# A recommender kernel with 16384 lookups a position: which tiles of rows are gathered whole, and which row by row

## The chip, the core and the metric

The kernel runs on one core of a Trainium2 chip. The metric is the device time of one execution in microseconds. The program is one launch: 200 history positions, then two small dense layers, all in float32.

## The reference

`B = 16384` samples, `L = 200` history positions, embeddings of `D = 64` floats (256 bytes a row). Cut to what is computed:

```python
it, c, u = i_emb[item], c_emb[cate], u_emb[user]        # each (B, 64)
h = i_emb[hist]                                         # (200, B, 64)
feat = concat([h, it, h - it, h * it])                  # (200, B, 256)
a = dice(feat @ au_W1 + au_b1, au_alpha, axis=1)        # 36 units; moments over the batch, for each l
w = a @ au_W2 + au_b2                                   # (200, B, 1)
cur = sum(w * h, axis=0)                                # (B, 64)
z = concat([u, it, c, cur])                             # (B, 256)
z = dice(z @ W1 + b1, alpha1, axis=0)                   # 80 units
z = dice(z @ W2 + b2, alpha2, axis=0)                   # 40 units
out = z @ W3 + b3                                       # (B, 2)
# dice(x) = x * (p + alpha * (1 - p)),  p = sigmoid((x - mean) / sqrt(var + eps))
```

The item, category and user tables are read by random index: 16384 rows for each of 200 positions, which is 3.3 million rows of 256 bytes.

## The kernel before

**Tiles and steps.** A tile is 128 samples (one row of the table for each partition). The batch is 128 tiles, cut in `ND = 8` groups of `TD = 16` tiles. A step `k = 8 l + c` handles group `c` of history position `l`: 16 tiles of rows are brought into `rows[k % 5]` (five buffers, L105), DVE turns them into `hT` by 32x32 blocks (L153, four instructions a step), PE multiplies, ACT evacuates `xs` (`hidden`, L372) and computes the sigmoid (`gate`, L361), DVE multiplies and adds to `curT` (L364, L368, L369). `gate`, `weights` and `weigh` of a step come `LAG = 9` steps late, when the moments of their position are known (`moments`, L403).

**Two ways of fetching rows.** A whole tile comes by one indirect DMA, which POOL issues from a column of 128 indices in SBUF (`gather`, L124; here "a gather"). For the groups in `SIDES = (1, 3, 4, 5, 6, 7)` the sixteenth tile can come by address instead: SP and ACT load 128 row addresses into registers, up to 24 at a time (L315), and each issues half of them as a DMA of 256 bytes (L323; here "a row DMA"), into one of three `side` buffers. DVE waits until all 128 have landed (`await_rows`, L342) and copies the tile into `rows` (`place_tile`, L385). `shares` (L293) spreads the row DMAs of a position evenly over its 8 steps: with 5 tiles by address each queue issues 40 a step, with 6 tiles 48. On ACT they stand between `hidden` and `gate` and behind `gate` (`step`, L423).

**How many tiles by address.** Five groups always have one; group 5 (`SOMETIMES`) has one where `l % EACH < MOST` (`has_side`, L348). With `EACH = 3` that is every third position. A position with 6 such tiles costs POOL 122 gathers, here "a six"; one with 5 costs 123 gathers, "a five". Before, the order is six, five, five.

**Stages.** (1) The start: the item rows are gathered, group by group, into `rows[c % 5]` and turned into `itT` (L538 to L554); with `ask_all` six tiles come by address, with 432 row DMAs on SP and 336 on ACT. Beside that the categories are looked up by matrix products: DVE compares (`pick_categories`, L498: 8 comparisons for each of 16 half groups), PE multiplies, ACT copies each half out of PSUM (L509), and ACT's queue loads and stores (`spread_categories`, `store_categories`). History step `k` fills `rows[k % 5]`, so step 0 needs the item group 5 turned, step 1 group 6. Memsets and copies end the stage (L556 to L566); `head_weights` (L246, 57 small DMAs on SP, then DVE operations that wait for them) is called last, and most of it is placed behind the loop. (2) The loop: 2 passes of `LPB = 90` positions (L570), with a barrier of all engines between passes and behind the last. (3) 20 positions more. (4) The users (L645 to L675): 8 groups, 122 + 1 gathers and 5 tiles by address, and the first dense layer for each group: `head_layer` multiplies category, item and `curT` (into `px`, 128 rows, and `ph`, 32 rows), then the user rows come in, and ACT evacuates (`head_units`). The last attention steps (`gate`, `weights`, `weigh`) run in between. (5) Two dense layers with moments over the whole batch (L677 to L750).

**Order.** `manual_schedule` keeps the order of the program on each engine within a region; the engines meet through semaphores alone.

Of the kernel before, what the change touches and what calls it, by code (L numbers as in the profile page):

```python
# [14 lines left out]
P = 128  # L15
# [12 lines left out]
EACH = 3  # L28
# [8 lines left out]
def din_kernel(  # L37
# [76 lines left out]
    ids = [make(f"ids{i}", P, NC, dt=I32) for i in range(2)]  # L114
    side = [make(f"side{i}", P, D) for i in range(3)]
# [117 lines left out]
    w2b = make("w2b", P, P)  # L233
    w3 = make("w3", P, 4, P)
    b1a = make("b1a", P, 1)
    b1b = make("b1b", S, 1)
# [9 lines left out]
    def head_weights():  # L246
# [9 lines left out]
        for g in range(2):  # L256

            nc.sync.dma_start(w1a[ts(g, D), 2, ts(g, ZA)], w1[:, 2, :ZA])
            nc.sync.dma_start(w1b[ts(g, D), 2, ts(g, ZB)], w1[:, 2, ZA:])
            nc.sync.dma_start(w2a[ts(g, ZA), g * ZA : g * ZA + Z2], W2[:ZA])  # L260
            nc.sync.dma_start(b1a[ts(g, ZA)], col(b1)[:ZA])
            nc.sync.dma_start(ala[ts(g, ZA)], col(alpha1)[:ZA])
            nc.sync.dma_start(b1b[ts(g, ZB)], col(b1)[ZA:])
            nc.sync.dma_start(bias2[g * ZA : g * ZA + Z2], col(b2))
            nc.sync.dma_start(al2[g * ZA : g * ZA + Z2], col(alpha2))
            for j in range(4):
                r = slice(j * S + g * ZB, j * S + (g + 1) * ZB)
                nc.sync.dma_start(w2b[r, g * ZA : g * ZA + Z2], W2[ZA:])
                w = j * S + g * ZO
                nc.sync.dma_start(w3[g * ZA : g * ZA + Z2, j, w : w + ZO], W3)  # L270
                nc.sync.dma_start(alb[r], col(alpha1)[ZA:])
        nc.sync.dma_start(bias3, b3.partition_broadcast(P))
# [64 lines left out]
    def ask_all(s, split, first, n, at, table):  # L337
        for queue, runs in enumerate(shares(NS * P // ND, s, split)):
            runs = [(r0, min(end, n * P)) for r0, end in runs if r0 < n * P]
            ask(queue, runs, first, range(n), at, table)  # L340

# [47 lines left out]
    def fetch_all(k, c, ids, table):  # L389
        for n in range(TD - (c in SIDES)):  # L390
            j = column(c, n)
            gather(rows[k % ROWS], ids[:, j : j + 1], n, table)
# [91 lines left out]
    def order_categories():  # L484
        for c in range(ND):
            n, j = TD - (c in SIDES), column(c, 0)
            nc.scalar.dma_start(cs[c][:, :n], columns(r_cate)[:, j : j + n])
            if c in SIDES:
                j = column(c, TD - 1)
                nc.scalar.dma_start(cs[c][:, n:], col(r_cate[j * P : (j + 1) * P]))  # L490
        nc.scalar.dma_start(table, c_emb.rearrange("(b p) d -> p b d", p=PB))
# [26 lines left out]
    with tc.manual_schedule():  # L518
        nc.sync.dma_start(ids[0], columns(r_item))
        load_addresses(2, r_item.rearrange("(o b) -> o b", o=1))  # L520
        nc.vector.memset(hm, 0.0)
        nc.scalar.copy(hT[SPREAD], hm)
        order_categories()
        load_hist_ids(0, 0)
        load_addresses(0, r_hist[0:1])
        nc.sync.dma_start(ids[1], columns(r_user))
        nc.gpsimd.iota(lanes, pattern=[[1, P]], base=P, channel_multiplier=-1)
        for q in range(SPREAD - 1):
            spread_categories(q)
# [4 lines left out]
        scale_addresses(2)  # L534
# [3 lines left out]
        for c in range(ND + 1):  # L538
            if c < ND:
                fetch_all(c, c, ids[0], i_emb)  # L540
                ask_all(c, 0.56, -NS, NS, addr[2], i_emb)
                for q in (2 * c, 2 * c + 1):
                    pick_categories(q)
                    if q + SPREAD - 1 < HALVES:
                        spread_categories(q + SPREAD - 1)
                    if q:
                        store_categories(q - 1)
            if c == 0:
                attention_weights()
                scale_addresses(0)  # L550
            if c:
                if c - 1 in SIDES:
                    place_tile(c - 1, SIDES.index(c - 1) - NS)
                transpose(itT[c - 1], rows[(c - 1) % ROWS])  # L554
# [12 lines left out]
        head_weights()  # L567
# [10 lines left out]
    zst = [make(f"zst{i}", P, n, STATS) for i, n in enumerate((2 * ND, 4, 2 * ND))]  # L578

    def measure_head(i, j, t, h):  # L580
        nc.vector.bn_stats(zst[i][:, 2 * j + h, :], t[:, ts(h, CH)])

# [34 lines left out]
    def head_layer(pairs):  # L617
        layer(px, [(w1a[:, f], t) for f, t in pairs], last=False)
        layer(ph[:S], [(w1b[:, f], t) for f, t in pairs], last=False)
# [6 lines left out]
    def head_units(c):  # L626
        evacuate(za[c], px, b1a, 0, c)
        if c == ND - 1:
            start_moments("z", 0, 2, 0, same_a)
        for h in range(2):  # L630
            nc.scalar.activation(
                zb[c // 4][ts(c % 4, S), ts(h, CH)], ph[:S, ts(h, CH)], AF.Identity, bias=b1b
            )
            if c % 4 == 3:
                measure_head(1, c // 4, zb[c // 4], h)

    with tc.manual_schedule():
        steps(BODY, L - BODY, L - BODY, r_user.rearrange("(o b) -> o b", o=1))
        U = addr[(L - BODY) % 3]
        j = column(SIDES[-1], TD - 1)  # L640
        nc.sync.dma_start(sidx[0], col(r_user[j * P : (j + 1) * P]))
        first = -(-tiles_by_address(L - BODY)[0] // 3) * 3

        weighed = {*range(-LAG, K - LAG), K, K + 1}
        for j in range(ND + 2):  # L645
            if j < ND:
                fetch_all(K + j, j, ids[1], u_emb)
                if j == SIDES[-1]:
                    gather(rows[(K + j) % ROWS], sidx[0], TD - 1, u_emb)
                nc.sync.dma_start(category[j % 2], catT[j])  # L650
            step(K + j, K - 1, weighed)
            weighed.add(K + j - LAG)
            left = [k for k in range(K) if k not in weighed]
# [5 lines left out]
            if j < ND:  # L659
                ask_all(j, SPLIT, first, NS - 1, U, u_emb)  # L660
            if 1 <= j <= ND:
                c = j - 1
                head_layer(((2, category[c % 2]), (1, itT[c]), (3, curT[c])))
                if c in SIDES[:-1]:
                    place_tile(K + c, first + SIDES.index(c))
                parts = (0, TD) if c < ND - 1 else (0, TD - 4, TD)
                for n in map(slice, parts, parts[1:]):
                    transpose(user[c % 2], rows[(K + c) % ROWS], n)
                    for dst, w in ((px, w1a[:, 0]), (ph[:S], w1b[:, 0])):
                        for i in range(2):  # L670
                            nc.tensor.matmul(
                                by_tile(dst, i)[:, n], w, by_tile(user[c % 2], i)[:, n],
                                start=False, stop=n.stop == TD, skip_group_check=True,
                            )
# [21 lines left out]

        beside = {0: range(4), 4: range(4, 6), 6: range(6, 8)}
        for c in range(ND + 2):
            if c < ND:
                if c % 4 == 0:  # L700
                    dice(ab[c // 4], zb[c // 4], nb, al1b, alb, 2 if c == 0 else 1, c > 0)
                for i in range(2):
                    for k in beside.get(c, ()):
                        r = ts(k % 4, S)
                        nc.tensor.matmul(
                            pz[k % 4][:, ts(i, CH)], w2b[r], ab[k // 4][r, ts(i, CH)],
                            start=True, stop=False, skip_group_check=True,
                        )
                dice(curT[c], za[c], na, al1a, ala, 2 if c == 0 else 1, c % 2 == 1)
                layer(pz[c % 4], [(w2a, curT[c])], first=False)  # L710
# [70 lines left out]
```

## Time and profile before

| what | before |
|---|---|
| median of 3 runs | 31195.79 us (31191.82 to 31199.41) |
| the profiled execution | 31199.79 us |
| its span, first to last instruction | 31198.0 us |
| POOL: busy, instructions | 23418.8 us (75%), 24783 |
| gathers: item, history, user | 122, 24533, 123 |
| PE, DVE, ACT busy | 67%, 50%, 12% |
| row DMAs on SP and on ACT | 69056 and 68928 |
| granted TensorE clock, mean | 0.809 |

The profiled execution lies 4.0 us above the median. The page counts only the execution of instructions as busy: the issuing of a DMA by SP or ACT, and POOL's time between two gathers, stand as idle. So POOL's 75% and ACT's 12% aren't the load of these engines. In the lists, "start us, us" are the start and length of a group of instructions, and the bracket holds the idle time before it and what ended it; "ACTq" and "SPq" are the queues' own instructions. A name stands without its buffer number.

### The profile page before, as it was taken

Reading aid. Unit: us, or ns where it says so; the run is one execution under the profiler, and the core shown is the slowest. Engines: PE = TensorE matmul, PEld = TensorE weight load, DVE = VectorE, ACT = ScalarE, POOL = GpSimd, SP = SyncE. Lnnn points to the kernel's source line nnn. Section 1 sums busy time; section 2 is a strip of 40 time slices with the busy share of each in tenths; the row PEclk is TensorE's granted clock in tenths of the full one; section 3 lists DMA queues with packets and bytes.
Section 4 is the critical chain, followed back from the end, with each engine's and each line's share of the span. In section 5 each row is a group of like instructions: output and inputs, shape, how many; then the busy total and the mean of one; then the engine's idle time right before and its main releaser. Section 6 shows DMA issues by size and latency. Waiting matters only on the chain.

```text
span 31198.0 us, 427397 instructions
## 1 busy us (share of the span) xinstructions
PE 20922.2 (67%) x39376; PEld 8551.5 (27%) x39376; DVE 15705.3 (50%) x21745; ACT 3823.8 (12%) x3330; POOL 23418.8 (75%) x24783
## 2 busy tenths in 40 slices
PE   5666666666666666666666666666666666666667
PEld 2222222222222222222222222222222222222222
DVE  4555554554555555555455455555555555545554
ACT  1111111111111111111111111111111111111111
POOL 6777777777777777777777777777777777777776
PEclk7888888888888888888888888887888888888888
DMA  2111111111111111111111111111111111111111
GB/s 41 29 29 29 29 29 29 29 29 29 29 29 29 29 29 29 29 29 29 29 29 29 29 29 29 29 29 29 29 29 29 29 29 29 29 29 29 29 29 30
DMA packets 1135469, 907.51 MB, mean 29 GB/s; under 512 B 730704, under 2 KB 730704, under 8 KB 1132426
## 3 DMA queue, kind: packets, MB, share of 16 engines
q0 software_dynamic: 792896, 813.51, 13.9%
q1 hardware_dynamic: 193404, 35.89, 0.8%
q10 hardware_dynamic: 146125, 30.64, 0.7%
q14 instruction: 2734, 22.39, 0.2%
q8 instruction: 310, 5.08, 0.1%
HBM read 873.55 MB, written 4.39 MB: 28 GB/s over the span
## 4 chain that ended last, share of the span: by engine, by line
POOL 32%; issue 12%; PE 5%; DMA 4%; DVE 2%; ACTq 1%; ACT 0%; DVEq 0%; POOLq 0%
POOL rows L125 32%; DMA rows<-in_L_rec_i_emb,idx 4%; PE px L158 2%; PE ph L158 1%; PE wb L158 1%; ACTq L323 1%; DVE hT L153 1%; DVE wb L368 0%; DVE curT L369 0%; ACT pg L361 0%; DVE st L377 0%; ACTq L315 0%; ACT xs L372 0%; DVE y L364 0%; DVE hm L400 0%
## 5 line engine op out<-in xcount | busy, mean ns | idle before, releaser
L125 POOL DMA_INDIRECT rows<-in_L_rec_i_emb,idx x24400 | 23038.6, 944 | 7542.4 <-issue 7198.7
L158 PE MATMUL ph<-hT,unit 128*128 128x512 f32 x6404 | 5928.7, 1077 | 9820.7 <-DVE hT L153 9820.2
L368 DVE SCALAR_TENSOR_TENSOR wb<-wb,au_bias,hT 128x1024 f32<-128x1024 f32 x1609 | 2080.3, 1293 | 9802.6 <-PE wb L158 9802.6
L158 PEld LDWEIGHTS ph<-hT,unit 128*128 128x128 f32 x6404 | 1747.3, 305 | 12865.9 <-DVE hT L153 12687.8
L153 DVE STREAM_TRANSPOSE hT<-rows 64x512 f32<-64x512 f32 x6404 | 4517.0, 705 | 1483.9 <-DMA rows<-in_L_rec_i_emb,idx 894.5
L158 PE MATMUL px<-hT,blk_h 128*128 128x512 f32 x6404 | 4125.0, 733 | 0.0
L372 ACT ACTIVATE xs<-px,au_bias 128x1024 f32<-128x1024 f32 x1602 | 1783.6, 1113 | 14375.2 <-PE wb L158 10720.9
L158 PE MATMUL wb<-y,blk_p 128*128 128x512 f32 x6436 | 3318.4, 597 | 246.6 <-DVE y L364 246.1
L361 ACT ACTIVATE pg<-xs,sh,rs 128x1024 f32<-128x1024 f32 x1609 | 1943.0, 1208 | 12481.6 <-issue 9985.6
L158 PE MATMUL px<-itT,blk_i 128*128 128x512 f32 x6404 | 3355.8, 606 | 0.0
L158 PE MATMUL wb<-xs,blk_x 128*128 128x512 f32 x6436 | 3300.5, 594 | 5.3 <-DVE curT L369 5.3
L158 PE MATMUL px<-hm,blk_m 128*128 128x512 f32 x6408 | 3011.2, 592 | 0.0
L400 DVE TENSOR_TENSOR hm<-ph,itT 128x1024 f32<-128x1024 f32 x1601 | 1960.6, 1225 | 1920.1 <-PE ph L158 1920.0
L364 DVE TENSOR_TENSOR y<-pg,xs 128x1024 f32<-128x1024 f32 x1609 | 1959.4, 1218 | 1293.7 <-ACT pg L361 1291.5
L158 PEld LDWEIGHTS px<-hT,blk_h 128*128 128x128 f32 x6404 | 1649.9, 258 | 2417.9 <-issue 2363.7
L377 DVE BATCH_NORM_STATS2 st<-xs 128x6 f32<-128x512 f32 x3204 | 2058.9, 685 | 60.8 <-ACT xs L372 17.1
L369 DVE TENSOR_TENSOR curT<-wb,curT 128x1024 f32<-128x1024 f32 x1609 | 1970.4, 1225 | 54.8
L158 PEld LDWEIGHTS px<-itT,blk_i 128*128 128x128 f32 x6404 | 1402.0, 219 | 2031.2 <-issue 2031.2
L158 PEld LDWEIGHTS wb<-y,blk_p 128*128 128x128 f32 x6436 | 1215.2, 191 | 1847.9 <-issue 1460.7
L158 PEld LDWEIGHTS wb<-xs,blk_x 128*128 128x128 f32 x6436 | 1224.6, 190 | 1551.9 <-issue 1544.4
L158 PEld LDWEIGHTS px<-hm,blk_m 128*128 128x128 f32 x6408 | 1217.4, 190 | 1532.9 <-issue 1520.3
L387 DVE COPY rows<-side 128x64 f32<-128x64 f32 x1079 | 235.7, 218 | 485.0 <-DMA side<-in_L_rec_i_emb 472.9
(184 smaller groups left out, 2044.3 us busy)
## 6 DMA issues: line engine op xcount, KB each, us to landing
side<-in_L_rec_i_emb SPq DMA_DIRECT2D x68720, 0.2 KB
side<-in_L_rec_i_emb ACTq DMA_DIRECT2D x68624, 0.2 KB
rows<-in_L_rec_i_emb,idx POOLq DMA_INDIRECT x24400
idx<-in_r_hist SPq DMA_DIRECT2D x200, 61.0 KB
hT<-cs ACTq DMA_DIRECT2D x16, 500.0 KB
side<-in_L_rec_u_emb SPq DMA_DIRECT2D x336, 0.2 KB
side<-in_L_rec_u_emb ACTq DMA_DIRECT2D x304, 0.2 KB
ucT<-catT SPq DMA_DIRECT2D x8, 512.0 KB
```

Source lines behind the costliest of these rows:

```text
L125: nc.gpsimd.indirect_dma_start(out=dst[:, n, :], out_offset=None, in_=table, in_offset=bass.IndirectOffsetOnAxis(ap=ids, axis=0),)
L153: nc.vector.transpose(by_tile(dst[ts(e, D)], i)[:, n], of[ts(i, D), n, ts(e, S)])
L158: nc.tensor.matmul(dst[:, ts(i, CH)], lhsT, rhs[:, ts(i, CH)], start=(first and j == 0), stop=(last and j == len(pairs) - 1), skip_group_c ...
L323: dma = issue.dma_start(side[m % 3].bitcast(U8)[p : p + 1], flat[ds(a, ROW)].rearrange("(o d) -> o d", o=1),).then_inc(landed[m % 3], 16)
L361: nc.scalar.activation(pg, xs[k % XR], AF.Sigmoid, bias=shifts[i], scale=rstds[i])
L364: nc.vector.tensor_mul(y, pg, xs[k % XR])
L368: nc.vector.scalar_tensor_tensor(wb, wb, au_bias2, hT[k % LAG], ALU.add, ALU.mult)
L369: nc.vector.tensor_add(curT[k % ND], wb, curT[k % ND])
L372: nc.scalar.activation(xs[k % XR], px, AF.Identity, bias=au_bias)
L377: nc.vector.bn_stats(stats[l % 3][:, 2 * c + i, :], xs[k % XR][:, ts(i, CH)])
L387: nc.vector.tensor_copy(rows[k % ROWS][:, TD - 1], side[m % 3])
L400: nc.vector.tensor_mul(hm, ph, itT[k % ND])
```

## The change

1. **Items whole.** All 128 item tiles are gathered by POOL; `ask_all` and the row DMAs of the items go. Column indices of the six tiles come by `load_all_ids`, six small DMAs on SP.
2. **The order of the start.** The loads of the category indices are interleaved with the first `spread_categories`; the loads of history position 0 move behind the attention weights; the user indices and `head_weights` move into the item loop, at group 2.
3. **Users.** 126 gathers and only two tiles by address (groups 3 and 5), all on SP. The loop has one round less. `head_layer` is split: category and item come before `gate`/`weights`/`weigh`, `curT` and user behind. Its 32-row part (`ph`) is packed: four products of 256 columns side by side in the four quarters of the partitions in place of two of 512 in one quarter, so that one ACT instruction of 128x256 evacuates it.
4. **The second layer** takes the packed part 256 columns at a time, each group for itself, behind the main product.
5. **`EACH = 2`**: the sixth tile comes by address in every second position. The order is six, five, six, five.

```diff
-EACH = 3
+EACH = 2
...
+    side_ids = [make(f"side_ids{i}", P, NS, dt=I32) for i in range(2)]
...
-    w2b = make("w2b", P, P)
+    w2b = make("w2b", P, 2, P)
...
-    b1b = make("b1b", S, 1)
+    b1b = make("b1b", P, 1)
...
-    def fetch_all(k, c, ids, table):
-        for n in range(TD - (c in SIDES)):
+    def load_all_ids(i, v):
+        for s in range(NS):
+            j = NC + s
+            nc.sync.dma_start(side_ids[i][:, s : s + 1], col(v[j * P : (j + 1) * P]))
+
+    def fetch_all(k, c, i, table, by_address=()):
+        for n in range(TD):
             j = column(c, n)
-            gather(rows[k % ROWS], ids[:, j : j + 1], n, table)
+            at = ids[i][:, j : j + 1] if j < NC else side_ids[i][:, j - NC : j - NC + 1]
+            if j - NC not in by_address:
+                gather(rows[k % ROWS], at, n, table)
...
-        load_addresses(2, r_item.rearrange("(o b) -> o b", o=1))
+        load_all_ids(0, r_item)
...
-        order_categories()
-        load_hist_ids(0, 0)
-        load_addresses(0, r_hist[0:1])
-        nc.sync.dma_start(ids[1], columns(r_user))
         nc.gpsimd.iota(lanes, pattern=[[1, P]], base=P, channel_multiplier=-1)
-        for q in range(SPREAD - 1):
-            spread_categories(q)
+        for c in range(3):
+            order_categories(c)
+        nc.scalar.dma_start(table, c_emb.rearrange("(b p) d -> p b d", p=PB))
+        for c in range(3, ND):
+            if c - 3 < SPREAD - 1:
+                spread_categories(c - 3)
+            order_categories(c)
...
             if c < ND:
-                fetch_all(c, c, ids[0], i_emb)
-                ask_all(c, 0.56, -NS, NS, addr[2], i_emb)
+                fetch_all(c, c, 0, i_emb)
...
             if c == 0:
                 attention_weights()
+                load_hist_ids(0, 0)
+                load_addresses(0, r_hist[0:1])
                 scale_addresses(0)
+            if c == 2:
+                nc.sync.dma_start(ids[1], columns(r_user))
+                load_all_ids(1, r_user)
+                head_weights()
             if c:
-                if c - 1 in SIDES:
-                    place_tile(c - 1, SIDES.index(c - 1) - NS)
                 transpose(itT[c - 1], rows[(c - 1) % ROWS])
...
-        head_weights()
...
-    def head_layer(pairs):
-        layer(px, [(w1a[:, f], t) for f, t in pairs], last=False)
-        layer(ph[:S], [(w1b[:, f], t) for f, t in pairs], last=False)
+    def head_layer(pairs, first=False, last=False, n=(0, TD)):
+
+        for i in range(2):
+            for j, (f, t) in enumerate(pairs):
+                nc.tensor.matmul(
+                    by_tile(px, i)[:, slice(*n)], w1a[:, f], by_tile(t, i)[:, slice(*n)],
+                    start=first and j == 0, stop=last, skip_group_check=True,
+                )
+        for j, (f, t) in enumerate(pairs):
+            for r in range(4):
+                n0 = r % 2 * TD // 2
+                of = slice(max(n[0], n0), min(n[1], n0 + TD // 2))
+                if of.start < of.stop:
+                    to = slice(of.start - n0, of.stop - n0)
+                    nc.tensor.matmul(
+                        ph[ts(r, S), :QH].rearrange("p (n t) -> p n t", t=S)[:, to],
+                        w1b[:, f], by_tile(t, r // 2)[:, of],
+                        start=first and j == 0, stop=last, skip_group_check=True,
+                    )
...
-        for h in range(2):
-            nc.scalar.activation(
-                zb[c // 4][ts(c % 4, S), ts(h, CH)], ph[:S, ts(h, CH)], AF.Identity, bias=b1b
-            )
-            if c % 4 == 3:
-                measure_head(1, c // 4, zb[c // 4], h)
+        nc.scalar.activation(others(c), ph[:, :QH], AF.Identity, bias=b1b)
+        nc.vector.bn_stats(zst[1][:, c, :], others(c))
...
+        tiles = [SIDES.index(c) for c in (3, 5)]
...
-        for j in range(ND + 2):
+        for j in range(ND + 1):
+            c = j - 1
             if j < ND:
-                fetch_all(K + j, j, ids[1], u_emb)
-                if j == SIDES[-1]:
-                    gather(rows[(K + j) % ROWS], sidx[0], TD - 1, u_emb)
+                fetch_all(K + j, j, 1, u_emb, tiles)
                 nc.sync.dma_start(category[j % 2], catT[j])
             step(K + j, K - 1, weighed)
             weighed.add(K + j - LAG)
+            runs = [(r0, r0 + LOAD) for r0 in (2 * LOAD * j, 2 * LOAD * j + LOAD)]
+            runs = [(r0, min(end, len(tiles) * P)) for r0, end in runs if r0 < len(tiles) * P]
+            ask(0, runs, first, tiles, U, u_emb)
+            if j:
+                head_layer(((2, category[c % 2]), (1, itT[c])), first=True)
...
-            if j < ND:
-                ask_all(j, SPLIT, first, NS - 1, U, u_emb)
-            if 1 <= j <= ND:
-                c = j - 1
-                head_layer(((2, category[c % 2]), (1, itT[c]), (3, curT[c])))
...
+            if j:
+                head_layer(((3, curT[c]),))
+                if c in SIDES and SIDES.index(c) in tiles:
+                    place_tile(K + c, first + tiles.index(SIDES.index(c)))
                 parts = (0, TD) if c < ND - 1 else (0, TD - 4, TD)
...
+                for n in zip(parts, parts[1:]):
+                    transpose(user[c % 2], rows[(K + c) % ROWS], slice(*n))
+                    head_layer(((0, user[c % 2]),), last=n[1] == TD, n=n)
...
-        beside = {0: range(4), 4: range(4, 6), 6: range(6, 8)}
...
-                layer(pz[c % 4], [(w2a, curT[c])], first=False)
+                layer(pz[c % 4], [(w2a, curT[c])], last=False)
+
+                for r in (0, 2, 1, 3):
+                    of = ts(r // 2, D)
+                    nc.tensor.matmul(
+                        pz[c % 4][:, ts(r, QH)], w2b[of, r % 2], ab[c // 4][of, ts(c % 4, QH)],
+                        start=False, stop=r % 2 == 1, skip_group_check=True,
+                    )
```

## The prediction

> **What bounds it now.** I read the page first, then what POOL waits for, then the start, one loop position and the end as timelines.
>
> ```profile
> PE 20922.2 (67%) x39376; PEld 8551.5 (27%) x39376; DVE 15705.3 (50%) x21745; ACT 3823.8 (12%) x3330; POOL 23418.8 (75%) x24783
> L125 POOL DMA_INDIRECT rows<-in_L_rec_i_emb,idx x24400 | 23038.6, 944 | 7542.4 <-issue 7198.7 <-DMA rows<-in_L_rec_i_emb,idx 155.2 <-DVE itT L153 83.3
> ```
>
> A gather is 944 ns, and 0.30 us of issue follow: in the timeline one starts 1.249 us after another (27841.19, 27842.44). The 24778 gathers at that pace are 30948 us of a span of 31198. So POOL's count sets the time; the other 250 us are a start, a barrier and an end where POOL stands still. In what POOL waits for, one row is large: DVE turning items, 83.6 us in 4 waits.
>
> ```profile
> 53.49 11.31 POOL L125 DMA_INDIRECT rows<-in_L_rec_i_emb,ids  x1 [0.30 <-issue]
> ...
> 245.98 0.94 POOL L125 DMA_INDIRECT rows<-in_L_rec_i_emb,idx  x1 [67.96 <-DVE itT L153]
> ...
> 280.71 0.94 POOL L125 DMA_INDIRECT rows<-in_L_rec_i_emb,idx  x1 [14.82 <-DVE itT L153]
> ```
>
> POOL's timeline of the start: the first two history steps wait for item groups 5 and 6. Why these are late stands on ACT and PE:
>
> ```profile
> 205.19 19.17 ACTq L323 DMA_DIRECT2D side<-in_L_rec_i_emb  x42
> 224.46 0.59 ACT L509 COPY ucT<-ph 128x512 f32<-128x512 f32 x1 [25.16 <-issue]
> ```
> ```profile
> 225.10 9.94 PE L505 MATMUL ph<-xs,curT 125*64 125x512 f32 x32 [19.57 <-ACT ucT L509]
> ```
>
> In every item group the copy out of PSUM queues behind 42 row DMAs, and PE waits for it, 18.5 to 19.8 us behind the first group.
>
> **1. The start.** History step 2 starts at 299.65 and POOL is unhindered from there. By then it has issued 122 + 31 gathers, at 1.249 us from 2.88 on, it would have been at 194: 105.5 us are lost. 82.4 of them are the waits above; 23.1 are slow item gathers (122 at a mean of 1133 ns against 944), which run beside DVE's comparisons. The change takes ACT's and SP's row DMAs out, so PE needs per group about 2 x 7.03 us (its row when it is not held up) and 0.9 for the copy: 15, in place of 35.5. `head_weights` now stands in group 2 and DVE waits for its 63 DMAs on SP; behind the loop 50 of them took 25.3 us (27856.60 to 27881.86), so 32 here; behind it on DVE stand the turning of item group 1, whose buffer POOL wants for group 6 at about 143, and the comparisons of group 3, for which PE and ACT wait. First comparison at about 17, groups 0 and 1 with the attention weights until 63 (64.6 now), group 2 until 80, `head_weights` until 114, and 15 to 16 a group: group 7 is done at about 190. POOL needs 128 x 1.249 and the slow gathers of 8 groups in place of 5, 23.1 x 8/5 = 37: history step 0 starts at 200, and no buffer is late. Net: 82.4 - 14 - 7.5 (six gathers) = **61 us saved**. Bounds: 75 without slow gathers beyond today's; 15 if every group's comparisons hold POOL as the 11.31 us gather was held (8 x 10.4 = 83 in place of 37). That gather lies over DVE's 16 comparisons of 54.01 to 64.68; beside comparisons that wait for PE the rows say 1.41. They will mostly wait for PE, so I take 37.
>
> On this place the Trainium skill has a rule (SBUF — State Buffer, "Who interferes with whom"): a VectorE operation in a two-port mode holds the port pair it shares with GpSimd for its whole length, and the other is blocked, not slowed. Read so, all eight groups would cost as the 11.31 us row does, and the saving would be near 15. The 1.41 us rows show that between two comparisons with a gap the gather slips in.
>
> DVE ends the stage 2.3 (landing) + 2.9 (turning) + 10.7 (memsets) behind POOL's last item gather: 216, now 311.8.
>
> **2. POOL's count.** Sixes become 100 of 200 instead of 67: 33 history gathers fewer, **41.2 us**. Users: three more, +3.7.
>
> **3. The attention chain.** Here the change may give back. In a six ACT has 8 more row DMAs a step:
>
> ```profile
> 10037.62 8.74 ACTq L323 DMA_DIRECT2D side<-in_L_rec_i_emb  x24
> 10046.41 1.21 ACT L361 ACTIVATE pg<-xs,sh,rs 128x1024 f32<-128x1024 f32 x1 [9.51 <-issue]
> 10048.33 8.22 ACTq L323 DMA_DIRECT2D side<-in_L_rec_i_emb  x24
> 10056.65 1.11 ACT L372 ACTIVATE xs<-px,au_bias 128x1024 f32<-128x1024 f32 x1 [9.03 <-DVE hT L153]
> ...
> 10142.26 1.21 ACT L361 ACTIVATE pg<-xs,sh,rs 128x1024 f32<-128x1024 f32 x1 [7.11 <-issue]
> 10143.91 6.80 ACTq L323 DMA_DIRECT2D side<-in_L_rec_i_emb  x20
> 10150.81 1.11 ACT L372 ACTIVATE xs<-px,au_bias 128x1024 f32<-128x1024 f32 x1 [7.34 <-PE wb L158]
> ```
>
> Its step is 20.1 us in a six (10046.41 to 10066.49) and 17.1 in a five (10142.26 to 10159.32); POOL's is 152.4/8 = 19.05 and 153.6/8 = 19.2. So in a six ACT, and DVE behind it, fall back, and in a five they catch up. Behind the start, where all are late, one sees the chain's own pace: gates of positions 6, 9, 12, 15 and 18 start at 1231.3, 1678.9, 2129.1, 2576.3 and 3027.3, 449.0 us for six, five, five, against POOL's 368 x 1.249 = 459.6. The five that the change leaves out measures 142.5 (position 7) to 144.6 (position 8). A six and a five are then 304.4 to 306.5; POOL's 245 gathers are **306.0**. Position 8's last step already holds four DMAs of the next six, position 7's doesn't, so the five to leave out is nearer to 142.5: I take 306.1 for the pair, a tie; the first two rounds (454.1, 453.5) put 9 us on top. So a lag of the chain, which now melts by 10 a round, stays.
>
> It costs nothing while POOL runs ahead (five buffers are 5 x 19.1 us, of which the step in hand takes some 25), but at the end of a pass all meet:
>
> ```profile
> 14053.49 0.94 POOL L125 DMA_INDIRECT rows<-in_L_rec_i_emb,idx  x1 [0.30 <-issue]
> 14059.99 0.94 POOL L125 DMA_INDIRECT rows<-in_L_rec_i_emb,idx  x1 [5.56 <-DVE rows L387]
> ```
>
> POOL waits the lag (1.7 us there, DVE's start on step 718 after its last gather) plus 3.8. With the change: DVE turns step 0 27.5 us behind the stage's end, at 243.5; POOL has it at 220, lag 23.5; the first six adds 12, a five's catching up takes 10 by its group 6, the slow rounds add 9, 44 pairs at 0.1 add 4: 38, **+37**. In the second pass the lag starts from the barrier, 17 after its first six now, 7 at the end of a five: +5 and 4, **+9**. Behind it `head_weights`, which holds DVE for 13.5 and 4.9 us at 27862 to 27883, is gone; POOL doesn't feel that today.
>
> SP is no bound: a six takes it 179.4 us with 25 of waits, a five 134, together 288 of 306.
>
> **4. Users and end.** Now PE sets the end, not POOL:
>
> ```profile
> 31053.72 5.15 PE px L158 x12
> 31058.87 5.27 PE ph L158 x12
> 31064.14 1.91 PE px L671 x4
> 31071.63 2.84 PE wb L158 x6
> ```
>
> A user step is 20.7 us on the chain (31053.72 to 31074.48), of which PE stands 3.7 waiting for the gate behind `px`. POOL's last gather ends at 31078.70, PE's last `px` product at 31123.49: 44.8 behind. With the change category and item products stand beside the gate, and `ph` is packed; four products with 32 rows start within 0.02 us of another at 31134.61 (L705), which speaks for side by side; if not, `ph` keeps its 7 us. A step is 13 to 18 us, under POOL's 20. Then the end is 2.3 (landing) + 0.9 (last four tiles) + 0.8 (products) behind POOL: 4.0, **40.8 saved**. One ACT and one DVE instruction for the packed part in place of two each, before the moments: 1.5 saved. The second layer stays with ACT and DVE.
>
> **Sum**: -61 - 41.2 + 3.7 + 37 + 9 - 40.8 - 1.5 = -95. The profiled execution becomes 31105; from the median of 31195.8 it is **31101 us**.
>
> **Rivals.** (a) *POOL alone binds*: a pair takes the chain 305.5 or less, the lag melts as now, at the barriers +5 at most: -136, 31060. For it: positions 6 and 7 took 303.0 (1231.3 to 1534.3). Against it: position 7 comes before a five there, with 20 DMAs in the next step's first batch and not 24. (b) *The chain binds*: a pair takes 306.5 to 308, and 88 pairs in the two passes add 0.4 to 1.9 us each at the barriers, 35 to 167 in all: 31136 to 31268. For it: positions 0 and 1 took 307.0, 3 and 4 took 308.6. It decides from 1.1 us a pair above the tie (95/88): from there the kernel is **slower** than before, with ACT's queue of row DMAs as the bound. (c) *The start keeps its loss*: POOL held in each group as in the 11.31 us row, 46 less: 31147. (d) *The change doesn't do what it says*: if the packed products don't run side by side, that costs under 5 us, since POOL covers them; if `head_weights` stayed behind the loop, the start's chain would be 32 shorter and POOL's time the same.
>
> **How the numbers follow.** The forecast (a pair from 0.5 below to 0.35 above the tie, 31060 to 31132) has 0.45; (a) 0.22; (b) 0.26, of which 0.20 lie within 0.2% of before and 0.06 beyond it on the slow side (from 157/88 = 1.8 us above the tie); (c) and (d) 0.07, within. 0.2% (62 us) is about what a measurement of this kernel can tell from no change. Faster by more: 0.45 + 0.22 = 0.67; within: 0.27; slower: 0.06. The range goes from (a) with a start that saves 75 and not 61, 31050 in round figures, to (b) at 306.9 a pair, 31175.
>
> **What will show it.** Right: no POOL wait of 68 us before history step 0, which starts near 200; DVE done with the stage near 216; gates of a six and a five 306 us apart; 24754 gathers; POOL's idle time at the barrier between the passes 25 to 60 us; in the user stage no PE product behind POOL's last gather but the last few. Wrong: that idle time under 10 (the chain catches up, rival a) or waits of POOL for `hT` inside a pass (rival b); gathers of 10 us in several item groups (c).

## The result, and the profile after

The changed kernel takes **31064.33 us** (median of 6 runs, 31054.04 to 31079.56), the kernel before on the same chip 31196.67 us (6 runs, 31191.82 to 31202.58): a ratio of 0.9958, with a 95% interval of 0.9946 to 0.9969. That is 132 us less. The forecast was 31101 in a range of 31050 to 31175, so the sign and the range held and the number was 37 us too high. The profiled execution of after is the slowest of its six (31079.56 us, span 31077.8, mean TensorE clock 0.815); its span is 120.2 us shorter than that of before.

The page of after, in the two lines that answer to those of before (busy time, share of the span, instructions; then the costliest group on POOL):

```profile
PE 20995.0 (68%) x39536; PEld 8516.2 (27%) x39536; DVE 15726.0 (51%) x21772; ACT 3816.6 (12%) x3322; POOL 23397.1 (75%) x24759
L126 POOL DMA_INDIRECT rows<-in_L_rec_i_emb,idx x24400 | 23039.7, 944 | 7492.3 <-issue 7196.8
```

POOL still sets the time, with 24 instructions fewer and the same 944 ns a gather. The idle time of the group no longer names `itT`. In what POOL waits for, the large row is another one now (sum, times, longest):

```profile
POOL rows L126 <- issue: 7301.5, 23911, 1.0
POOL rows L126 <- DVE rows L383: 37.4, 16, 30.3
```

The 83.6 us of waits for turned items are gone, and one wait of 30.3 us stands at the barrier between the passes. The start, on POOL's timeline (start, length, and in the bracket the idle time before it and what ended it):

```profile
44.67 11.88 POOL L126 DMA_INDIRECT rows<-in_L_rec_i_emb,ids  x1 [0.30 <-issue]
...
175.67 1.41 POOL L126 DMA_INDIRECT rows<-in_L_rec_i_emb,ids  x1 [0.30 <-issue]
...
185.65 0.94 POOL L126 DMA_INDIRECT rows<-in_L_rec_i_emb,idx  x1 [0.30 <-issue]
```

History step 0 starts 1.25 us behind the last item gather, without a wait, at 185.65. On ACT, the copies out of PSUM that stood behind 42 row DMAs before:

```profile
120.22 0.58 ACT L510 COPY ucT<-wb 128x512 f32<-128x512 f32 x1 [44.24 <-PE wb L506]
...
128.00 0.59 ACT L510 COPY ucT<-wb 128x512 f32<-128x512 f32 x1 [7.19 <-PE wb L506]
...
134.86 0.59 ACT L510 COPY y<-px 128x512 f32<-128x512 f32 x1 [6.28 <-PE px L506]
```

They now wait for PE, and come 7 to 8 us apart: the pace of PE's 7.1 us for each half of a group, as the prediction had it. The 44.24 us are `head_weights`: DVE waits 27.7 and 6.8 us for its DMAs (L275), and PE and ACT stand still with it. POOL's timeline at the two barriers (at 13942.91 its last gather of step 718, at 13961.64 its last of the pass):

```profile
13942.91 0.94 POOL L126 DMA_INDIRECT rows<-in_L_rec_i_emb,idx  x1 [0.30 <-issue]
...
13961.64 0.94 POOL L126 DMA_INDIRECT rows<-in_L_rec_i_emb,idx  x1 [0.30 <-issue]
13992.92 0.94 POOL L126 DMA_INDIRECT rows<-in_L_rec_i_emb,idx  x1 [30.34 <-DVE rows L383]
```
```profile
27781.65 0.94 POOL L126 DMA_INDIRECT rows<-in_L_rec_i_emb,idx  x1 [2.84 <-DVE rows L383]
```

What POOL waits for at the first one is on DVE's timeline, the last whole step of the pass (718):

```profile
13973.74 2.88 DVE L154 STREAM_TRANSPOSE hT<-rows 64x512 f32<-64x512 f32 x4
...
13988.22 1.29 DVE L364 SCALAR_TENSOR_TENSOR wb<-wb,au_bias,hT 128x1024 f32<-128x1024 f32 x1 [6.83 <-PE wb L159]
13989.55 1.22 DVE L365 TENSOR_TENSOR curT<-wb,curT 128x1024 f32<-128x1024 f32 x1
13992.18 0.20 DVE L383 COPY rows<-side 128x64 f32<-128x64 f32 x1 [1.41 <-PEq L573]
```

DVE starts on step 718 at 13973.74, 29.9 us behind the end of POOL's last gather of that step (13943.85); this distance is called the lag here. POOL had issued its last gather of the pass at 13961.64, when DVE was a step and a half behind; DVE works until 13990.8, the barrier opens, and both go on at 13992. And the end, before and after:

```profile
31122.78 0.71 PE L671 MATMUL px<-ucT,w1a 128*128 128x128 f32 x4
```
```profile
30998.56 0.94 POOL L126 DMA_INDIRECT rows<-in_L_rec_u_emb,side_ids  x1 [0.30 <-issue]
...
31002.31 0.49 PE L629 MATMUL px<-ucT,w1a 128*128 128x128 f32 x2 [0.17 <-DVE ucT L154]
31002.73 0.41 PE L639 MATMUL ph<-ucT,w1b 128*32 128x128 f32 x4
```

PE's last `px` product ends 3.3 us behind the end of POOL's last gather (30999.50), where it ended 44.8 us behind before (31123.49 against 31078.70).

### The profile page after: what moved, and what is told of

Read it like the earlier page. It is cut to its first block, busy times and chain, and to the rows that moved or that the text cites. A ratio compares the mean times of both kernels' runs of the same rounds, so it can differ in the third digit from the quotient of the medians.

```text
span 31077.8 us, 433840 instructions
## 1 busy us (share of the span) xinstructions
PE 20995.0 (68%) x39536; PEld 8516.2 (27%) x39536; DVE 15726.0 (51%) x21772; ACT 3816.6 (12%) x3322; POOL 23397.1 (75%) x24759
## 3 DMA queue, kind: packets, MB, share of 16 engines
q14 instruction: 2780, 22.77, 0.2%
## 5 line engine op out<-in xcount | busy, mean ns | idle before, releaser
L159 PE MATMUL wb<-y,blk_p 128*128 128x512 f32 x6436 | 3394.3, 609 | 762.7 <-DVE y L360 762.3
```

The costliest lines, as they stand in the source:

```text
L159: nc.tensor.matmul(dst[:, ts(i, CH)], lhsT, rhs[:, ts(i, CH)], start=(first and j == 0), stop=(last and j == len(pairs) - 1), skip_group_c ...
```

## The experiments

**What was to be told apart.** The theory of the prediction: a six and a five together take the chain as long as they take POOL (306 us), so the lag that the start leaves isn't melted any more and is paid at the first barrier; of the 41 us that `EACH = 2` takes from POOL, 25 come back there. The rival: POOL's count alone decides, the 41 us are gained whole, and the 30 us at the barrier have another cause.

The chips were not alike: two of the twelve experiments ran on a chip that takes 31202.75 us for the kernel before (number 10, here "a 31 ms chip"), ten on chips that take 50784 to 51150 us for the same kernel (numbers 7, 15 and 8, here "51 ms chips"). So there are two groups, and each kernel is compared with the kernel before on its own chip.

### POOL slowed, on a 31 ms chip

The chain can't be made faster in one stroke, but POOL can be made slower: twelve gathers more in each step, into buffers that nobody reads.

```diff
+    spare = [make(f"spare{i}", P, PAD, D) for i in range(2)]
...
             gather(rows[k % ROWS], ids, n, i_emb)
+        for n in range(PAD):
+            gather(spare[k % 2], idx[l % IDX][:, n : n + 1], n, i_emb)
```

`PAD = 12`, once with `EACH = 2` and once with `EACH = 3`.

> The changed kernel (sixth tile in every second position) with twelve gathers more in each history step, whose rows go to spare buffers and are used by nobody. In the runs above ACT's and SP's instructions came late and the chain took 507 us a pair (gates, changed kernel), so POOL stood behind it all the time and the gathers saved could not show. With 245 + 192 gathers a pair POOL takes 546 us and is the bound again, with 39 us of slack a pair. 24754 + 19200 gathers at 1.2515 us are 55009 us, with the start (85 us lost), the end (150) and two barriers: 55250 to 55330 us. Theory (where the chain has slack its lag melts): POOL's idle time at each barrier falls from 93.6 and 88.1 us to under 45 us, the lag of the last step as before plus 0.4 us. Rival (the idle time at the barrier has nothing to do with slack): 80 to 95 us again.

> The same twelve extra gathers a step with the sixth tile in every third position: 33 history gathers more than with every second. Theory: with slack in the chain the count alone decides, so this kernel is 33 x 1.25 = 41 us slower than the one with every second (25 to 55), and not 16 us as the count and the barrier together made it where the chain ties with POOL. Rival (the sixth tile costs the chain something even with slack, for instance through the DMA queues): within 15 us of it, or faster.

Measured: **55012.02 us** with every second (5 runs, 55010.96 to 55048.53) and **55051.88 us** with every third (5 runs, 55049.86 to 55052.51); beside the kernel before 1.7632 (1.7608 to 1.7656) and 1.7644 (1.762 to 1.7668). The first lies some 240 us under the least that was expected, since that was worked out for a 51 ms chip; with the terms of the 31 ms chips the sum closes: 43954 gathers x 1.249 = 54899, start 25 (185.1 less 128 x 1.249), barriers 11, 80 from the last gather on, 55015. The difference between the two is 39.9 us, where 33 gathers are 41.2: **with slack in the chain, the count is gained whole**. POOL at the first barrier, with every second and with every third:

```profile
24770.90 0.94 POOL L128 DMA_INDIRECT rows<-in_L_rec_i_emb,idx  x1 [8.25 <-DVE rows L387]
```
```profile
24772.25 0.94 POOL L128 DMA_INDIRECT rows<-in_L_rec_i_emb,idx  x1 [9.49 <-DVE rows L387]
```

The barrier itself, the rest of the code and the start are those of the changed kernel; only POOL's pace differs, and the wait falls from 30.3 to 8.3 us. Part of that fall is trivial: the last twelve extra gathers of a pass stand between POOL's last useful gather and the barrier, and give the chain 15 us there. The lag itself tells more. DVE starts on step 0 18.7 us behind POOL's last gather of that step that is used, as in the changed kernel (18.6); one position later it stands at 1.5 us with the twelve extra gathers, and at 31 us without them, and at step 718 at 2.2 us against 29.9. The 8.3 us that are left are no lag: DVE itself stands idle 37 us at that barrier.

```profile
24770.18 0.20 DVE L387 COPY rows<-side 128x64 f32<-128x64 f32 x1 [37.34 <-PEq L577]
```

So the 30.3 us are the lag, and the lag stays because POOL leaves the chain no slack. This stands against the rival.

The other half, the same lag with a six in every third position and POOL at its usual pace, can be read from the profile of before, whose loop differs from that of after by `EACH` alone. There the lag at the sixes of positions 0, 3, 6, 9, 12, 15 and 18 is 73, 55, 48, 36, 26, 14 and 6 us, and then 4 to 6 to the end of the pass. In after it is 30 at position 6 and 25 to 32 at every six behind it. So six, five, five melts a lag of 73 us in 18 positions, and six, five doesn't melt one of 30 in 84. What no run measures is the time: the 16 us that `EACH = 2` is worth on this start (41.2 less 24.8 at the barrier) are worked out from the two profiles.

### The sixth tile, alone and elsewhere, on the 51 ms chips

Four edits were meant to measure that. All four ran on 51 ms chips, three of them twice or more, so that none of them met the condition they were made for.

The changed kernel with `EACH = 3`:

> The changed kernel with the sixth tile in every third position again (start and users stay changed). Theory (the chain of a six and a five ties with POOL's 306 us, so the lag that the start leaves isn't melted and is paid at the barrier): six, five, five lets the lag melt by 10 us a round, POOL's idle time at the barrier between the passes falls from 30.3 to 5 to 7 us; 33 history gathers come back (41.2 us), 25 go at the barrier: 31064 + 41 - 25 = 31080 us (31072 to 31090). So the sixth tile would be worth some 16 us and not 41. Rival (POOL's count alone decides, and the 30 us at the barrier have another cause): the barrier stays near 30 us and the time is 31064 + 41 = 31105 us.

Measured: 50976.53 us (6 runs) against 51126.46: 0.9969 (0.9957 to 0.9981).

The kernel before with `EACH = 2` and nothing else, on three chips:

> The kernel before, with nothing but the sixth tile in every second position. Theory: the old start leaves the chain 73 us behind, a pair of positions doesn't melt it, so POOL waits some 65 to 75 us at the first barrier in place of 5.56, and now and then for turned buffers inside the first pass: 31197 - 41 + 65 (plus 5 to 10 in the first pairs) = 31225 us (31205 to 31235), slower than before. Rival (POOL's count alone decides): 31197 - 41 = 31156 us, with the barrier under 20 us.

> The kernel before, with nothing but the sixth tile in every second position, once more, since a row DMA took twice its time in the runs above (0.75 us on SP against 0.40) and SP's queue was the bound in all of them. Where a row DMA takes its usual 0.40 us, theory (the chain ties with POOL, its lag isn't melted): the old start leaves the chain 73 us behind, POOL waits some 65 to 75 us at the first barrier in place of 5.56, and at times for turned buffers inside the first pass: 31197 - 41 + 65 (plus 5 to 10 in the first pairs) = 31225 us (31205 to 31235), slower than before. Rival (POOL's count alone decides): 31156 us, with the barrier under 20 us.

> The kernel before with nothing but the sixth tile in every second position, on a chip that runs the kernel before in 31.2 ms. Theory (a six and a five together take the chain what POOL takes, 306 us, so the 73 us by which the old start leaves the chain behind are not melted): POOL waits 60 to 75 us at the first barrier in place of 5.56, and at times for turned buffers in the first positions: 31200 - 41 + 65 = 31224 us, with up to 10 for the first pairs 31234 (31205 to 31235). Rival (POOL's count alone decides): 31159 us, the first barrier under 20 us. If it is slow again: +670 us as in the two runs there.

Measured: 51793.27 us (ratio 1.0127, 1.0111 to 1.0142), 51822.67 us (1.0128, 1.0111 to 1.0145) and 51503.59 us (1.0135, 1.0119 to 1.015): 667, 672 and 667 us slower, 20.2 us for each of the 33 positions.

Fives in place of the first sixes of a pass:

```diff
+    skipped = [2, 4, 6]
+
+    def sixth(l):
+        return l % EACH < MOST and l not in skipped
...
-        return c in SIDES and (c != SOMETIMES or l % EACH < MOST)
+        return c in SIDES and (c != SOMETIMES or sixth(l))
```

> The changed kernel with fives at positions 2, 4 and 6 of each pass in place of sixes, then a six in every second position as before; six gathers more in all (7.5 us). Theory: four fives in a row melt the lag of 22 us at position 2 by about 10 us each until it stands where the second pass has it (5 to 6 us at the start of a six), and it stays there; POOL's idle time at the first barrier falls from 30.3 to 3 to 8 us: 31064 + 7.5 - 25 = 31047 us (31040 to 31055), faster than both kernels. Rival (the lag comes back within the pass, since the pair takes the chain longer than POOL): the barrier is at 20 to 30 us again, 31064 + 7.5 - 5 = 31066 to 31072 us.

> The changed kernel with fives at positions 2, 4 and 6 of each pass, six gathers more in all (7.5 us), on a chip that runs the kernel before in 31.2 ms. Theory: with POOL at 19.2 and the chain at 17.8 us a step in a five, the lag of 22 us melts by about 10 us in each of them until it stands at the 5 to 6 us of the second pass, and then it stays, since sixes and fives tie: POOL's idle time at the first barrier falls from 30.3 to 3 to 8 us; 31064 + 7.5 - 25 = 31047 us (31040 to 31058), faster than both kernels. Rival 1 (the lag comes back within the pass, a pair takes the chain longer than POOL): the barrier at 20 to 30 us, 31066 to 31072 us. Rival 2 (POOL's count alone decides): 31072 us.

Measured: 51521.61 us (1.0073, 1.006 to 1.0087) and 51205.36 us (1.0073, 1.0059 to 1.0087).

Row DMAs moved from ACT to SP, with larger loads of addresses in the same edit, so the two can't be told apart:

```diff
-LOAD = 24
-SPLIT = 0.5
+LOAD = 26
+SPLIT = 0.52
```

> The changed kernel with 52% of the row DMAs on SP and 48% on ACT (50 and 46 of a step of a six, 42 and 38 of a five; up to 26 addresses to a load). Theory: ACT's queue is what paces the chain, so a pair takes it 32 row DMAs at 0.34 us less, 295 in place of 306 us; the lag melts by 10 us a pair, POOL's idle time at the first barrier falls from 30.3 to 3 to 8 us: 31064 - 25 = 31039 us (31030 to 31048). Rival 1 (DVE or PE paces the chain, not ACT's queue): the barrier stays at 25 to 30 us, 31060 us. Rival 2 (SP is the bound with 32 DMAs more a pair, 288 + 13 = 301 us by its timeline, close to POOL's 306): DVE waits for landed side tiles, POOL for turned buffers, and the time rises above 31100 us.

> The changed kernel with 52% of the row DMAs on SP and 48% on ACT (50 and 46 in a step of a six, 42 and 38 in a five; up to 26 addresses to a load), on a chip that runs the kernel before in 31.2 ms. Theory (ACT's queue of row DMAs paces the chain): a pair takes ACT 32 row DMAs at 0.34 us less, 295 in place of 306 us, the lag melts by up to 10 us a pair and the first barrier falls from 30.3 to 3 to 8 us: 31064 - 25 = 31039 us (31030 to 31050). Rival 1 (DVE or PE paces the chain): the barrier at 25 to 30 us again, 31060 us. Rival 2 (SP, at 288 + 13 = 301 us of work a pair, is now the bound): DVE waits for side tiles, POOL for turned buffers inside the passes, and the time rises above 31100 us.

Measured: 56076.95 us (1.0971, 1.0953 to 1.0988) and 55749.37 us (1.0971, 1.0956 to 1.0986).

None of the expectations for a 31 ms chip holds here, because they don't speak of the bound that these chips have; the one sentence that does, 670 us for the sixth tile alone once more, came out (667). The bound is not POOL: its gather is 943 to 946 ns there too. What differs first of all are the queues of SP and ACT. SP's row DMAs in the middle of the first pass, in the kernel before on a 31 ms chip and in the changed kernel with `EACH = 3` on chip 7 (start, length of the group, count):

```profile
9999.87 41.37 SPq L323 DMA_DIRECT2D side<-in_L_rec_i_emb  x104
```
```profile
10000.40 153.91 SPq L324 DMA_DIRECT2D side<-in_L_rec_i_emb  x206
```

That is 0.40 us a row against 0.75. In the trace most of them come at the usual pace of 0.32 us, but in stretches of some 15 us many instructions on the queue start 0.70, 1.40 or 2.10 us behind the one before: also the register moves ahead of each row DMA. Of SP's moves none takes more than 0.05 us in the kernel before, in after and in the kernels with twelve extra gathers on a 31 ms chip; on the 51 ms chips 12 to 14% of them take more than 0.4 us, most of these 0.70 (the median is 0.03 on both). In these runs the chain is so slow that POOL waits for a turned buffer in 1371 to 1474 of the 1600 steps, and the lag stands at 115 to 170 us in the pass (up to 192 with the split); so the slack that was to melt it isn't there, and the theory can't be tested. One figure bears on it all the same: with DVE 88 to 101 us behind in the last whole step of a pass, POOL waits 84 to 104 us at the barriers of all nine of these traces (the changed kernel of the next section among them). A lag is paid there whatever made it.

Open stay, for a 31 ms chip: the times of the sixth tile alone with the old start, of `EACH = 3` in the changed kernel, of the later sixes (which the theory makes 17 us faster than the changed kernel), and of the 52 to 48 split.

### The changed kernel, and no row DMAs, on a 51 ms chip

The changed kernel once more, and one with all tiles of the history gathered whole (1100 gathers more, no row DMAs in the loop):

```diff
-        return c in SIDES and (c != SOMETIMES or l % EACH < MOST)
+        return c in BY
```

with `BY = ()` and the index columns of the six tiles loaded for every position.

> The changed kernel itself once more, beside the others. Where a row DMA takes 0.32 to 0.40 us on SP: 31064 us (31050 to 31080), with 15 to 35 us of POOL's idle time at the first barrier, the lag of that execution. Where SP's and ACT's instructions come in bursts at 0.70 us: the sixth tile in 33 more positions cost 667 and 672 us alone there (20.2 us a position), start and users alone -150 us; if these add up, 51126 + 670 - 150 = 51645 us (51600 to 51690), slower than before by 1%. Rival there (the parts don't add, since the bound is not the count of row DMAs): within 0.2% of before.

> The changed kernel with no history tile by address: POOL gathers all 128 tiles of each position, 1100 gathers more than the changed kernel, and ACT and SP issue no row DMAs in the loop. Theory for the pace: 31064 + 1100 x 1.249 = 32438 us, and since ACT's queue is empty the lag melts at once and the first barrier falls from 30 to 3 to 8 us: 32413 us (32400 to 32430). The same on every chip, also on those of the runs above, where SP's and ACT's instructions come in bursts at 0.70 us each and the kernel before took 51126 us: without row DMAs nothing of that is left, so the kernel is 37% faster there. Rival (the slow chips hold POOL too, through the tables or the DMA engines): well above 33000 us there. Rival on the barrier (the 30 us have nothing to do with ACT's queue): the first barrier is at 25 to 35 us again.

The changed kernel took **51235.06 us against 50784.1** (1.0088, 1.0075 to 1.0102): **slower than before**, by 451 us (the interval is 381 to 518), where the parts gave 670 - 150 = 520. They add up within their intervals (the 150 is 97 to 220). What POOL waits for in it:

```profile
POOL rows L126 <- DVE hT L154: 19902.6, 1379, 35.8
```

19.9 ms of waiting for turned buffers, which the prediction named as the sign of rival (b), the chain as the bound. On such a chip a tile by address costs more (20.2 us) than the gather that it saves (1.25), and the change adds tiles by address.

Without row DMAs the time is 41587.1 us (0.8187, 0.8174 to 0.8199). The expectation of 32413 failed by 9 ms: 18% are gained, not 37%, and POOL still waits 9.1 ms for turned buffers (797 waits). The time is the expectation's rival, well above 33000 us, but not by its cause: a gather stays at 946 ns. With no row DMA on any queue in the loop, the chain itself comes to a stop every second step. ACT and DVE in that kernel:

```profile
9995.06 1.20 ACT L361 ACTIVATE pg<-xs,sh,rs 128x1024 f32<-128x1024 f32 x1
10024.66 1.11 ACT L372 ACTIVATE xs<-px,au_bias 128x1024 f32<-128x1024 f32 x1 [28.40 <-issue]
```
```profile
10003.80 1.21 DVE L364 TENSOR_TENSOR y<-pg,xs 128x1024 f32<-128x1024 f32 x1
10028.16 1.29 DVE L368 SCALAR_TENSOR_TENSOR wb<-wb,au_bias,hT 128x1024 f32<-128x1024 f32 x1 [23.15 <-remote]
```

In these 28 and 23 us neither does anything, and PE, for whose products both wait, is done at 10011.9, 12.7 and 16.2 us before they go on; no recorded work ends the wait. Then comes a step of 18 us at the usual pace. So slow row DMAs are not the whole of it: it looks as if on these chips the engines get to their next instruction late. That is a reading of the traces; no run tests it, and its cause is not settled. Why the split costs 9.7% there is open too.

## Why the prediction was right, and where its sizes were off

Term by term, from the two profiled executions (no other run of after has a profile, so whether the burst is in others too isn't known):

| term of the sum | predicted | measured |
|---|---|---|
| start | -61 | -75.3 |
| 33 history gathers, 3 user gathers | -41.2, +3.7 | -41.2, +3.7 |
| first barrier, POOL's idle time | +37 (42) | +24.8 (30.3) |
| second barrier | +9 | 0 (2.84, before 2.86) |
| end behind POOL's last gather | -42.3 | -41.0 (78.3, before 119.3) |
| a burst of late gathers | not thought of | +10.1 |
| sum | -95 | -119, of -120.2 by the spans |

Without the burst the terms are -129, and the medians differ by -132, so the other five rows come to within 3 us of the measured change. The range of 31050 to 31175 took in rivals (a) and (c) and a part of (b), so that the time lay in it says little. What tells the forecast from its rivals is its sign, POOL's idle time at the first barrier: 25 to 60 us were named, under 10 for (a), and it is 30.3.

**The start, right in kind, mis-sized by 14.** "History step 0 starts at 200": it started at 185.65. All of it is one term, "23.1 x 8/5 = 37" for slow item gathers, which came to 22.9. The two bounds were 23 and 83 and I took 37, by scaling with the number of groups; the near bound was right. So the saving of 75 is the bound that was called "without slow gathers beyond today's". One gather is held about as long as before (11.88 us, 11.31 before), beside the 16 comparisons of item group 1, and the others cost 12.0 together. The comparisons of groups 1 and 2, and a gather beside the latter:

```profile
45.06 10.67 DVE L502 TENSOR_SCALAR xs<-hT,values 125x1024 f32<-125x1024 int32 x16
```
```profile
58.55 10.70 DVE L502 TENSOR_SCALAR xs<-hT,values 125x1024 f32<-125x1024 int32 x16
```
```profile
61.08 1.02 POOL L126 DMA_INDIRECT rows<-in_L_rec_i_emb,ids  x1 [0.30 <-issue]
```

The held gather lies from 44.67 to 56.55 on POOL, the comparisons of group 1 from 45.06 to 55.73. The two kernels with twelve extra gathers repeat it: step 0 at 185.1 and 185.9, one gather held 10.4 and 10.5 us longer than its pace. But the reason that the prediction gave for 37, that the other comparisons "will mostly wait for PE", failed: in after 91 of the 127 comparisons behind the first start less than 0.70 us after the one before, so they wait for nothing, against 24 in before. And these are the cheap ones. The gathers beside them mostly take 1.02 us (1.31 at the start of a group), those beside comparisons that come at PE's pace, 0.86 us apart, 1.41 or 1.42. So eight groups cost no more than the groups of before did, because most comparisons stopped waiting for PE. That rival (c) failed all the same was luck, as far as the reason goes.

The Trainium skill's rule (SBUF — State Buffer, "Who interferes with whom") has the two engines lock each other out of a shared port pair for the length of an operation. The held gather would fit such a lock if it were kept over sixteen operations, but the gathers beside group 2, whose comparisons come as close together (10.70 us for 16), are not held. Why the one gather is held and the others aren't, no run shows.

**The count, right.** 24754 gathers, and 39.9 us for 33 of them where the chain has slack.

**The tie, right; the lag, 8 us too large.** The step of the working was "a lag of the chain, which now melts by 10 a round, stays". In after the lag is 18.6 us at step 0, 22, 26 and 30 at positions 2, 4 and 6, and then 29 to 32 at the sixes' starts until position 46, 25 to 31 behind that, and 29.9 at step 718. It was to begin at 23.5 and end at 38: the start gave 5 less (DVE was done earlier as well), the slow first pairs 11 as forecast, and the 44 pairs "at 0.1 add 4" nothing. At the barrier "plus 3.8" was wrong on top: POOL waited 0.4 us more than the lag. Rival (a), POOL alone, came out at 31060 and so nearer to the measured 31064 than the forecast, but not for its reason: its mark was an idle time under 10 us at the barrier, and that is 30.3.

**The second barrier, wrong by 9.** I let the lag of the second pass grow from the first six on and forgot what I had used for the first barrier: the last position of a pass is a five, and in it the lag falls. In after it is 5 to 7 at the starts of the sixes (from the fourth on) and 1.5 at step 1438, behind the closing five (1.7 before the change).

**The end, right.** 40.8 and 1.5, together 42.3, were worked out, and 41.0 came; the packed products start four at a time, eight of them in 0.64 us.

The six times of after spread over 25 us, those of before over 11, and those of the changed kernel with twelve extra gathers over 2 without the profiled one. That fits a lag that differs from run to run and is paid at the barrier, but only one execution of after was profiled, so it isn't shown.

## What to carry to other kernels

When work is moved off the engine that sets the pace, ask what slack it leaves to the chain behind it: here a lag from the start cost nothing as long as the chain had slack to melt it, and the whole of it at the next barrier once chain and POOL tied. To find out which part of a wait is such a lag, slow the leading engine down by a known amount and see whether the lag, and not only the wait, goes. And a gain that trades one queue for another holds where the queues cost what they cost: the same change was 0.4% faster on one chip and 0.9% slower on another, so measure on more than one before a close trade is kept.

## What the hardware showed that I had not expected

**Chips differ by 63 to 64% on one program.** It takes 31.2 ms on chip 10 and in the first comparison, 50.8 to 51.2 ms on chips 7, 15 and 8, on chip 8 both times. The gather of POOL (0.944 and 0.946 us), DVE's and ACT's instructions have the same durations on both; what differs is when SP, ACT and, it seems, the others get to their next instruction: on SP some 1400 stretches of 15 us in the changed kernel (1260 to 1650, by where one lets a stretch end), about one for each 107 instructions, 24 ms or more of 51.2. The Trainium skill (Runtime: NRT & Kernel Launch, "Instruction fetch mechanics") says that an engine's instructions are brought in by blocks while the ones before run, and that the cost of passing from block to block is mostly hidden. On the 31 ms chips that agrees with the traces, where none of SP's register moves takes over 0.05 us; on the others something of this kind may not stay hidden. No run here shows that it is the fetching: the packets on the queue that the profile lists as "q14 instruction" are as many (2780), and take the same time, 0.41 us in after and 0.42 in the changed kernel on chip 8 (medians).

**A burst.** In the profiled execution of after 26 gathers between 14380 and 14487 us start 1.29 to 2.15 us after one another in place of 1.249, 10.1 us in all. The profile names the landing of an earlier gather as what POOL waits for (28 waits, 17.1 us, in that stretch):

```profile
14426.38 0.95 POOL L126 DMA_INDIRECT rows<-in_L_rec_i_emb,idx  x1 [1.09 <-DMA rows<-in_L_rec_i_emb,idx]
```

The last of a gather's 16 landings comes 9.6 us behind the gather's end in that stretch (median), and 2.6 us behind it around 10000 us; each gather waits on the semaphore of the gather eight before it, and eight gathers take 10.0 us. So gathers landed late for 100 us, once; why, no run shows. POOL's median pace is 1.250 us in the profiled execution of the kernel with twelve extra gathers and `EACH = 2`, 1.249 in that with `EACH = 3`: over 44000 gathers that is as much as the effect that was to be measured, and their profiled spans differ by only 4.0 us (55046.7 and 55050.7), where the medians differ by 39.9. The times of the other executions are what the 39.9 us rest on.
